# Writing the fourth chunk's result into the neighbouring image's slot, and storing five chunks with one DMA

## The chip, the cores and the metric

The kernel runs on one NeuronCore of a Trainium2 chip. The metric is the device time in microseconds (us) of one execution. Five engines work side by side, each through its own list of instructions in order: PE (matrix products), DVE (elementwise work), ACT (activation functions), POOL (elementwise work, and a queue of DMAs) and SP (a queue of DMAs). They meet through semaphores alone. A DMA is issued by an engine's queue (SP or POOL here) and carried out by 16 DMA engines that all queues share; its completion is counted on a semaphore, on which a later instruction can wait.

## The reference

Two layers are added to an image batch `x` of 16 images, 128 channels, 64 x 64 pixels, in float32. The first is a diagonal LSTM over the group-normalised input. The second, in which the change lies, is a 1 x 1 convolution through a simulated four-qubit circuit:

```python
x = x + _L0_conv_ref(_gn(x), ...)          # diagonal LSTM
x = x + _L1_conv_ref(_gn(x), ...)

def _L1_conv_ref(x, pre_w, pre_b, q_weights, post_w, post_b):
    xq = xf @ pre_w.T + pre_b              # 128 channels -> 4 angles per pixel
    z = _simulate(xq, q_weights)           # 4 qubits, 2 layers -> 4 expectations
    out = z @ post_w.T + post_b            # 4 -> 128 channels
    ...
```

The result has the shape of `x`: 16 images of 128 x 4096 float32, 2 MB each.

## The kernel before

**Where the data lies.** The 128 channels are the 128 partitions. An image's 4096 pixels are eight chunks of 512 (`CHUNK`), numbered k = 0 to 7 in the order of its rows. On the chip, `ring` (line 111) holds for each of the 16 images 40 of the 64 rows, that is five chunks of 2 KB a partition. Its rows are turned: `place` (line 140) puts k = 4, 5, 6, 7 into the first four chunks of an image's slot, and k = 3 into the fifth and last. So within one image's slot k = 3 lies behind k = 7. As the slots lie one behind the other, the last chunk of image b-1's slot lies directly in front of image b's k = 4. The three lower chunks (k = 0, 1, 2; `NT` is 3) do not fit and wait in a DRAM tensor `low` (line 114). They are brought back into buffers that come free: first into those of the first stage, then, as images are finished, into the places of their k = 4, 5, 6 in `ring` (`freed`, `load`, lines 1071 to 1088).

**The stages.** First the input is loaded and its statistics are taken. Then comes a scan of 160 steps (`NSTEP`), which takes most of the time. The last stage begins about 1277 us after the start of the span and handles the images one after another. It is written out by hand (`tc.manual_schedule()`, line 1233), so each engine works in the order in which the code emits instructions. The loop at line 1272 does this for image b:

- `outputs(b, 0)`: four matmuls on PE, each with 32 rows of the array, into four PSUM banks of a pool of five (`ps_o`, line 1060): results `po` for k = 0 to 3.
- `finish(b, 0)`: for each k one DVE instruction (line 1196) adds the bias and the old value and writes the sum back over that old value; then its store is issued, where one is due (line 1207, SP's queue).
- `load()`: loads of lower chunks for later images, on POOL's queue, for each buffer that came free.
- `sines(b + 2)` in two parts: ACT and one DVE instruction (line 1151); between the parts `squares(b + 1)`: two PE matmuls (line 1162) and two squares on ACT (line 1175).
- `outputs(b, 1)` and `finish(b, 1)`: the same for k = 4 to 7.
- `angles(b + 3)`: eight PE matmuls (line 1120) that read all eight chunks of image b + 3.
- In the last images, where no angles are left, `idle` puts two matmuls in their place whose results nobody reads.

**Which stores go together.** `together` (line 1216) says how many chunks one store carries. From image 5 to image 14 an image makes three stores: k = 0 to 2 in one (768 KB; two stores for image 5, whose three lie in two buffers), k = 3 alone (256 KB), and k = 4 to 7 in one (1024 KB). In the last image k = 4 to 7 go as two stores of 512 KB. A DMA on SP's queue uses one of eight completion semaphores in turn, and waits for the DMA eight before it.

Of the kernel before, what the change touches and what calls it, by code (L numbers as in the profile page):

```python
# [13 lines left out]
ALU = mybir.AluOpType  # L14
# [3 lines left out]
NB = 16  # L18
NH = 64
NW = 64  # L20
# [3 lines left out]
RING = 40  # L24
ROWS = 4
BLOCK = ROWS * NW
CHUNK = 2 * BLOCK
# [55 lines left out]
def kernel(  # L83
# [16 lines left out]
    nc = tc.nc  # L100
    xv = x.rearrange("b c h w -> b c (h w)")
    ov = out.rearrange("b c h w -> b c (h w)")
# [8 lines left out]
    ring = const.tile([P, NB, RING * NW], F32, name="ring")  # L111
    NLOW = NH - RING
    NT = NLOW * NW // CHUNK
# [24 lines left out]
    b_out = const.tile([P, 1], F32, name="b_out")  # L138

    def place(r):  # L140

        return (r + AHEAD if r < SLOTS else r - SLOTS) * NW

    def block(r):

        return ring[:, :, place(r) : place(r) + BLOCK]
# [18 lines left out]
    with ExitStack() as scan:  # L165
# [68 lines left out]
        with ExitStack() as prep:  # L234
# [37 lines left out]
            def behind(b):  # L272
# [10 lines left out]
                out=qw, in_=q_weights.rearrange("l w a -> (l w a)").partition_broadcast(P)  # L283
# [703 lines left out]
        with tc.manual_schedule():  # L987
# [26 lines left out]
            v = block(NH - ROWS).rearrange("p i (r w) -> p i r w", w=NW)[:, :, :, NW - STRIP :]  # L1014
# [55 lines left out]
    begun = {5: (last[:, 1:2], 1)}  # L1070
    freed, loaded = [], [len(groups)]

    def load():

        while freed and loaded[0] < NB:
            b = loaded[0]
            groups[b] = freed.pop(0)
            k = 0
            if b in begun:
                v, k = begun[b]  # L1080
                groups[b] = [(groups[b][0][0][:, k:], NT - k)]
            for v, n in groups[b]:
                of = low[b, :, k * CHUNK : (k + n) * CHUNK]
                nc.gpsimd.dma_start(out=v, in_=of.rearrange("p (k n) -> p k n", n=CHUNK))
                k += n
            if b in begun:
                groups[b].insert(0, begun[b])
            loaded[0] += 1

    def low_group(b, k):  # L1090

        for v, n in groups[b]:
            if k < n:
                return v, n, k
            k -= n

    def rows_of(b, k):
        if k < NT:
            v, _, i = low_group(b, k)
            return v[:, i]  # L1100
        at = place(2 * ROWS * k)
        return ring[:, b, at : at + CHUNK]

    def half(v, c):

        if c is None:
            return v
        return v[:, c * BLOCK : (c + 1) * BLOCK]
# [68 lines left out]
    def outputs(b, h, c=None, js=range(4)):  # L1177
        po = []
        for j in js:
            po.append(half(bank(ps_o, f"po{b}_{h}_{j}_{c}"), c))  # L1180
            k = 32 * j
            nc.tensor.matmul(  # L1182
                po[-1],
                lhsT=w_out[k : k + 32, :],
                rhs=half(sqs[b][h], c)[k : k + 32, :],
                start=True,
                stop=True,
                tile_position=(k, 0),
            )
        return po  # L1190

    def finish(b, h, po, c=None):
        for j in range(4):
            k = 4 * h + j
            v = rows_of(b, k)
            nc.vector.scalar_tensor_tensor(half(v, c), po[j], b_out, half(v, c), ALU.add, ALU.add)  # L1196
            n = together(b, k)
            if (k + 1) % n == 0 if k >= NT else n == 1 or n == low_group(b, k)[2] + 1:
                o = ov[b, :, (k + 1 - n) * CHUNK : (k + 1) * CHUNK].rearrange("p (k n) -> p k n", n=CHUNK)
                if k >= NT:  # L1200
                    at = place(2 * ROWS * (k + 1 - n))
                    to = ring[:, b, at : at + n * CHUNK].rearrange("p (k n) -> p k n", n=CHUNK)
                else:
                    to = v.unsqueeze(1) if n == 1 else low_group(b, k)[0]
                if c is not None:
                    o, to = (u[:, :, c * BLOCK : (c + 1) * BLOCK] for u in (o, to))
                nc.sync.dma_start(out=o, in_=to)
            if c != 0:
                if k == NT - 1 and len(groups[b]) == 1:
                    freed.append(groups[b])  # L1210
                if k == 7:
                    at = place(8 * ROWS)
                    v = ring[:, b, at : at + NT * CHUNK]
                    freed.append([(v.rearrange("p (k n) -> p k n", n=CHUNK), NT)])

    def together(b, k):

        if k < NT:
            return low_group(b, k)[1] if b > 1 else 1
        if k == NT:  # L1220
            return 1
        return 2 if b < 4 or b == NB - 1 else 4
# [10 lines left out]
    with tc.manual_schedule():  # L1233
# [15 lines left out]
        angles(1, 1, th, (0,))  # L1249
        po = outputs(0, 0, 0)  # L1250
        finish(0, 0, po, 0)
        squares(0, 1)
        angles(1, 1, th, (1,))
        ths[1, None] = th
        po = outputs(0, 0, 1)
        finish(0, 0, po, 1)
        load()
        later = sines(1)
        next(later)
        th = angles(2, parts=(0,))  # L1260
        po = outputs(0, 1, 0)
        finish(0, 1, po, 0)
        next(later, None)
        angles(2, None, th, (1,))
        po = outputs(0, 1, 1)
        finish(0, 1, po, 1)
        load()
        later = sines(2)
        next(later)
        squares(1)  # L1270
        next(later, None)
        for b in range(1, NB):
            po = outputs(b, 0)
            if b == 1:
                finish(b, 0, po)
                load()
                squares(2)
                th = angles(3, parts=(0,))
                po = outputs(b, 1)
                angles(3, None, th, (1,))  # L1280
                finish(b, 1, po)
                load()
                later = sines(3)
                next(later)
                next(later, None)
                continue
# [9 lines left out]
            po = outputs(b, 1)  # L1296
# [43 lines left out]
```

## Time and profile before

| what | value |
|---|---|
| three runs | 1395.71, 1396.30, 1396.86 us, median 1396.3 |
| profiled execution, its own time | 1396.12 us |
| its span, first to last instruction | 1394.3 us |
| mean granted TensorE clock | 0.994 |
| 1304 to 1390 us of the span: busy PE / DVE / ACT / POOL | 78.98 / 77.49 / 34.50 / 4.23 of 86.00 us |
| 1304 to 1390 us: what the DMA engines moved | 36.11 MB, 420 GB/s |
| stores of 1024 KB there, issue to landing (median) | 13.1 us |
| first stores of the stage (128 KB), issue to landing | 1.7 to 1.8 us |

The span is what the profiler saw between the first and the last instruction; the execution's own time has 1.8 us around it. Times inside the span are given from its start. A DMA's time to landing runs from its issue until the last of the 16 engines has counted its share; with a long queue most of it is waiting behind earlier DMAs. "Busy" for PE takes modelled ends of matmuls, so it says little about how full the array is. The clock is given as a share of full speed.

### The profile page before, as it was taken

To read this page: it belongs to the slowest core of one execution; us is meant where nothing else is said; L and a number is where in the kernel's file an instruction comes from. 1 tells how busy PE (TensorE), PEld (TensorE's weight loads), DVE (VectorE), ACT (ScalarE), POOL (GpSimd) and SP (SyncE) were. 2 spreads that over 40 slices of the span, in tenths; PEclk is the share of its full clock that TensorE was granted. 3 is DMA by queue.
4 is the path that set the end of the run, shared out by engine and by line. 5 is a ranking of instruction groups with operands and counts; after the bars stand their busy time and mean duration, and the time that the engine had idled before them with its cause. 6 is when DMAs were issued, how large, how long until landed. Compare 5 with 4: busy or idle time off the path is not lost. (4 is left out here: it accounts for less than half of the span.)

```text
span 1394.3 us, 19810 instructions
## 1 busy us (share of the span) xinstructions
PE 1348.3 (97%) x6058; PEld 966.7 (69%) x6058; DVE 970.3 (70%) x2509; ACT 796.1 (57%) x1896; POOL 876.3 (63%) x1560
## 2 busy tenths in 40 slices
PE   7888999999999999999999999999999999999996
PEld 6668878777777777767777777777777778886332
DVE  6973565577767776677777776666665566876996
ACT  6765666555555555555555555555555556655542
POOL 3236777776666677777777776777777667664000
PEclk9999999999999999999999999999999999999998
DMA  9950000000000000133333100000000000013999
GB/s 370 418 204 1 2 1 1 1 1 1 1 1 1 0 1 1 61 122 122 121 121 121 61 1 0 1 1 0 1 1 1 1 0 1 1 31 129 373 420 376
DMA packets 47674, 107.02 MB, mean 77 GB/s; under 512 B 2976, under 2 KB 30656, under 8 KB 44496
## 3 DMA queue, kind: packets, MB, share of 16 engines
q1 hardware_dynamic: 44928, 95.17, 18.1%
q0 software_dynamic: 2496, 10.58, 2.1%
q8 instruction: 48, 0.79, 0.2%
q14 instruction: 58, 0.48, 0.1%
q10 hardware_dynamic: 144, 0.01, 0.0%
HBM read 59.61 MB, written 46.14 MB: 76 GB/s over the span
## 5 line engine op out<-in xcount | busy, mean ns | idle before, releaser
L694 PE MATMUL ps<-trio,wxT 128*128 128x512 f32 (+18 forms) x1280 | 479.6, 518 | 0.6 <-POOL trio L685 0.6
L888 DVE TENSOR_TENSOR ps<-ps,both 128x256 f32<-128x256 f32 (+9 forms) x536 | 219.8, 410 | 295.4 <-PE ps L873 291.1
L892 ACT ACTIVATE ps<-ps,bias 128x512 f32<-128x512 f32 (+23 forms) x480 | 279.2, 583 | 219.4 <-DVE ps L888 183.1
L694 PEld LDWEIGHTS ps<-trio,wxT 128*128 128x128 f32 x1280 | 230.9, 190 | 173.2 <-issue 155.5
L873 PE MATMUL ps<-trio,w1T 128*128 128x256 f32 (+14 forms) x1088 | 306.3, 363 | 0.0
L873 PE MATMUL ps<-trio,w0T 128*128 128x256 f32 (+14 forms) x1088 | 305.5, 362 | 0.0
L923 ACT COPY both<-ps 128x256 f32<-128x256 f32 (+9 forms) x536 | 189.8, 356 | 180.9 <-PE ps L873 161.4
L873 PEld LDWEIGHTS ps<-pair,wsT 128*128 128x128 f32 x1088 | 196.0, 190 | 78.7 <-DVE pair L958 30.4
L873 PE MATMUL ps<-pair,wsT 128*128 128x256 f32 (+14 forms) x1088 | 243.5, 365 | 1.6 <-DVE pair L958 1.3
L731 POOL TENSOR_TENSOR ring<-ring,pair 128x256 f32<-128x256 f32 (+15 forms) x375 | 232.0, 646 | 18.2 <-DVE pair L958 17.9
L873 PEld LDWEIGHTS ps<-trio,w1T 128*128 128x128 f32 x1088 | 201.6, 190 | 22.3
L873 PEld LDWEIGHTS ps<-trio,w0T 128*128 128x128 f32 x1088 | 201.1, 190 | 21.2
L685 POOL TENSOR_TENSOR trio<-trio,rstd 128x512 f32<-128x512 f32 (+10 forms) x160 | 171.1, 1070 | 14.2 <-DVE rstd L529 1.7
L679 POOL TENSOR_TENSOR trio<-ring 128x256 f32<-128x256 f32 (+13 forms) x165 | 140.4, 851 | 0.0
L952 ACT ACTIVATE g<-cst 128x256 f32<-128x256 f32 (+20 forms) x320 | 103.0, 368 | 64.1 <-DVE cst L951 63.5
L958 DVE TENSOR_TENSOR pair<-g,ps 128x256 f32<-128x256 f32 (+17 forms) x319 | 105.4, 368 | 44.3 <-ACT g L952 39.4
L721 POOL TENSOR_TENSOR trio<-pair 128x240 f32<-128x240 f32 (+9 forms) x136 | 102.9, 757 | 36.6 <-DVE pair L958 33.0
L673 POOL TENSOR_TENSOR trio<-ring,mean 128x256 f32<-128x256 f32 (+15 forms) x191 | 123.3, 646 | 2.5 <-DVE mean L518 2.0
L978 POOL COPY trio<-pair 128x16 f32<-128x16 f32 x64 | 21.1, 330 | 148.7 <-DVE pair L958 148.7
L892 ACT ACTIVATE g<-ps,bias 128x512 f32<-128x512 f32 (+20 forms) x160 | 97.4, 609 | 27.6 <-DVE ps L888 21.4
L951 DVE TENSOR_TENSOR cst<-cst,ps 128x256 f32<-128x256 f32 (+20 forms) x320 | 104.4, 367 | 5.5
L948 DVE TENSOR_TENSOR ps<-ps,g 128x512 f32<-128x512 f32 (+20 forms) x160 | 95.0, 594 | 18.7 <-ACT g L892 18.5
(389 smaller groups left out, 1226.0 us busy)
## 6 DMA issues: line engine op xcount, KB each, us to landing
ring<-in_x_dram SPq DMA_DIRECT2D x13, 1024.0 KB, 9.8
low<-ring SPq DMA_DIRECT2D x6, 2048.0 KB, 7.6
ring<-in_x_dram SPq DMA_DIRECT2D x6, 2048.0 KB, 8.0
out_dram<-ring SPq DMA_DIRECT2D x11, 1024.0 KB, 13.1
trio<-in_x_dram SPq DMA_DIRECT2D x7, 768.0 KB, 7.6
rest<-in_x_dram SPq DMA_DIRECT2D x7, 768.0 KB, 7.7
ring<-low POOLq DMA_DIRECT2D x7, 768.0 KB, 8.9
out_dram<-ring SPq DMA_DIRECT2D x7, 768.0 KB, 12.7
```

What stands on the lines that cost most here:

```text
L673: op = nc.gpsimd.tensor_sub(by_pairs(xn, 0, j0, j1), x0, over(mean1, j1 - j0))
L679: op = nc.gpsimd.tensor_sub(by_pairs(xn, 1, j0, j1), lower, of)
L685: nc.gpsimd.tensor_mul(v, v, r)
L694: nc.tensor.matmul(ps[g][:, :, a:b], lhsT=wxT[:, g * 128 : (g + 1) * 128], rhs=xns[t % 2][:, :, a:b], start=t > 0, stop=True, skip_group_c ...
L731: op = engine.tensor_add(x1, x1, by_pairs(new, q, j0, j1))
L873: nc.tensor.matmul(out, lhsT=w[:, g * 128 : (g + 1) * 128], rhs=rhs, start=False, stop=True, skip_group_check=True,)
L888: nc.vector.tensor_add(v, v, both[g][:, a:b])
L892: nc.scalar.activation(to[:, :, a:w], ps[g][:, :, a:w], FUNC[g], bias=bias[:, g : g + 1])
L923: nc.scalar.copy(both[g][:, a:b], ps[g][:, 0, a:b])
L951: nc.vector.tensor_add(c[:, q], c[:, q], ig[:, q])
L952: nc.scalar.activation(th[:, q, a:w], c[:, q], AF.Tanh)
L958: nc.vector.tensor_mul(new[:, q, a:v], th[:, q, a:v], act[GO][:, q, a:v])
```

## The change

For the images 5 to 14 (`joined`), DVE's result for k = 3 no longer goes back over its own old value in the fifth chunk of image b's slot, but into the fifth chunk of image b-1's slot. There it stands directly in front of k = 4 to 7 of image b. k = 3 has no store of its own any more; when k = 7 is done, one DMA of 1280 KB stores k = 3 to 7, 10240 contiguous bytes a partition on both sides. Images 0 to 4 and 15 are as before.

```diff
     begun = {5: (last[:, 1:2], 1)}
     freed, loaded = [], [len(groups)]
 
+    flat = ring.rearrange("p b n -> p (b n)")
+    size = RING * NW
+    joined = {b: flat[:, b * size - CHUNK : b * size + (7 - NT) * CHUNK] for b in range(5, NB - 1)}
+
     def load():
...
         for j in range(4):
             k = 4 * h + j
             v = rows_of(b, k)
+            if b in joined and k == NT:
+                to = joined[b][:, 0:CHUNK]
+                nc.vector.scalar_tensor_tensor(to, po[j], b_out, v, ALU.add, ALU.add)
+                continue
             nc.vector.scalar_tensor_tensor(half(v, c), po[j], b_out, half(v, c), ALU.add, ALU.add)
             n = together(b, k)
-            if (k + 1) % n == 0 if k >= NT else n == 1 or n == low_group(b, k)[2] + 1:
+            if b in joined and k == 7:
+                nc.sync.dma_start(out=ov[b, :, NT * CHUNK : 8 * CHUNK], in_=joined[b])
+            elif (k + 1) % n == 0 if k >= NT else n == 1 or n == low_group(b, k)[2] + 1:
                 o = ov[b, :, (k + 1 - n) * CHUNK : (k + 1) * CHUNK].rearrange("p (k n) -> p k n", n=CHUNK)
```

The numbers and kinds of instructions on PE, DVE, ACT and POOL are the same in both programs; SP issues ten DMAs less. Semaphore waits are put in by the framework, from which instruction touches which bytes.

## The prediction

> **What bounds the kernel now.** The change touches the last stage alone, so I first read the table of stretches there, with the DMA columns; one row is a stretch of the span, its length, busy time of each engine, the granted clock, the DMA engines' share and GB/s.
>
> ```profile
> 1304.00:1390.00 86.00, 78.98 (x428) 27.07 (x424) 77.49 (x117) 34.50 (x58) 4.23 (x8) 0.96 1.02 420
> 1389.00:1390.70 1.70, 0.00 (x0) 0.00 (x0) 0.00 (x0) 0.00 (x0) 0.00 (x0) 0.50 0.85 346
> ```
>
> From 1304 to 1390 us the DMA engines are never idle. PE stops at 1383 and DVE at 1385.1 (its last eight operations start at 1379.74 and take 5.36 together), yet DMA goes on. SP's waits say how long:
>
> ```profile
> SPq L1336 <- DMA out_dram<-ring: 6.9, 1, 6.9
> ```
>
> So the span ends with the landing of the last store. It is issued at 1385.12 and lands 7.86 us later, at 1392.98; 1.3 us behind it the span ends. The first stores of the stage, of 128 KB, land in 1.7 us. What would the last one take without a queue before it? The trace's DMA packets give the service: a row of 2048 bytes holds its engine for 84 ns, 4096 for 159, 6144 for 234, 8192 for 309, that is 9 ns and 75 ns per 2 KB, and each DMA has 8 rows per engine and a 4-byte packet of 9 ns. Image 15's stores (768, 256, 512 and 512 KB, the first issued at 1381.83) therefore take 1.88 + 0.68 + 1.28 + 1.28 = 5.1 us; with a fixed 1.4 us (1.7 less 8 rows of half a 2 KB row, about 0.37 us) they would land at 1381.83 + 5.1 + 1.4 = 1388.4. **The store queue is thus 4.6 us behind the engines at the end** (1392.98 - 1388.4). This is the number to beat: engines that run up to 4.6 us later cost nothing, as long as the queue stays fed.
>
> What paces the engines is the next question. The timeline of DVE around image 5 (start, duration, operation; in brackets the idle time before it and who ended it):
>
> ```profile
> 1317.76 0.75 DVE L1196 SCALAR_TENSOR_TENSOR last<-po_None,b_out,last 128x512 f32<-128x512 f32 x1 [0.23 <-PE po_None L1182]
> 1318.42 1.40 DVE L1196 SCALAR_TENSOR_TENSOR trio<-po_None,b_out,trio 128x512 f32<-128x512 f32 x2
> 1319.74 0.74 DVE L1196 SCALAR_TENSOR_TENSOR ring<-po_None,b_out,ring 128x512 f32<-128x512 f32 x1
> 1320.40 0.68 DVE L1151 SCALAR_TENSOR_TENSOR y<-near_None,y 128x512 f32<-128x512 f32 x1
> 1321.00 2.72 DVE L1196 SCALAR_TENSOR_TENSOR ring<-po_None,b_out,ring 128x512 f32<-128x512 f32 x4
> 1323.94 2.73 DVE L1196 SCALAR_TENSOR_TENSOR ring<-po_None,b_out,ring 128x512 f32<-128x512 f32 x4 [0.23 <-PE po_None L1182]
> ```
>
> An image takes 6.18 us (1317.76 to 1323.94), with 0.23 us of idle DVE. PE is in the same loop: `po` of k = 0 to 3 is ready 1.16 us after its start, three DVE operations (2.07) free the bank for the eighth `po`, that takes 1.1, and the angles 1.85; the sum is 6.18. So neither engine can catch up by more than a fraction of 0.23 us an image.
>
> **What the change does, part by part.** *Ten stores less on SP.* A row of 10240 bytes costs 9 + 5 x 75 = 384 ns by the line above, against 84 + 309 = 393 for the two rows, so per engine and image 8 x 9 ns, and 9 for the packet that counts the completion: 81 ns, 0.8 us over ten images. No row that long is in the trace. If it is cut into 8192 and 2048, 0.1 us is left; if into five of 2048, it costs 420 ns and DMA loses 10 x (8 x 27 - 9) ns = 2.1 us. I take -0.8, as four lengths lie on the line. SP's own time, 0.33 us an issue, is hidden: it spends 38.1 us waiting for DVE here.
>
> *k = 3 is stored 4.1 us later* (1324 instead of 1320): behind stores that take 13 us to land this starves nobody. The buffers that come free for loads (k = 4 to 6) hung on the 1024 KB store and hang on the 1280 KB one, which is at the same place of the queue. The loads of images 14 and 15, issued at 1338.6 and 1340.8, land by 1352.1; the angles of 14 read them at about 1358, so they have 6 us of cover, and the delay below moves both.
>
> *A DVE operation writes elsewhere.* It keeps its 0.74 us: `last`, `trio` and `ring` targets all have it. For images 6 to 14 the chunk written over is the old k = 3 of the image before, whose readers are PE's angles and DVE's own earlier operation; it no longer has a store of its own. **For image 5 it is the place from which image 4's k = 3 is stored**, and this is new: the program of the changed kernel shows a wait for that store's semaphore on this operation, and on no other k = 3. The listing of this one store:
>
> ```profile
> L1207 SPq DMA_DIRECT2D out_dram<-ring x1: 951/951/951, 1314.3 to 1314.3; - x1
> ...
> DMA to landing us min/median/max: 10.7/10.7/10.7
> ```
>
> Issued at 1314.32, it lands at 1325.06. DVE wants to write at 1319.74: **5.3 us of standstill**. Nothing ahead of that store changes, so its landing is as certain as the queue's state. Behind the waiting instruction on DVE stand line 1151 of image 7, for which ACT waits with image 6's squares, and the four operations of k = 4 to 7. PE has banks for image 5's upper four and finishes image 8's angles at 1322.8; then it waits: the banks come free only from 1325.8 on, and the squares of image 6 need line 1151 (done 1326.5) and 0.6 us of ACT. So PE stands from 1322.8 to 1327.1. Walking on with the durations above, DVE begins image 6 at 1329.2 (before: 1323.94), image 7 at 1335.3 (1330.13) and then stays 5.2 us late. DMA has work meanwhile: at 1325 image 4's 1024 KB, image 5's 768 KB and loads 10 to 12 are still in the queue, and stores issued at 1319.85 land at 1333; it falls idle only in the images after, 1 us at a time, as it runs out of backlog.
>
> Against the 4.6 us of cover this alone is 1388.4 + 5.2 = 1393.6, or +0.6 us.
>
> *The clock of PE.* What does PE do after 4.3 us of standstill? The same table, in stretches of 6.83 us, the step on which all the clock's changes in this trace lie:
>
> ```profile
> 4.67:11.49 6.82, 4.28 (x30) 3.66 (x29) 3.65 (x7) 3.81 (x12) 5.79 (x18) 1.00 1.01 369
> 11.49:18.32 6.83, 4.53 (x20) 4.15 (x21) 5.71 (x10) 2.82 (x10) 0.38 (x3) 0.50 1.06 402
> 18.32:25.15 6.83, 5.59 (x40) 4.69 (x40) 5.62 (x10) 5.89 (x24) 1.49 (x5) 1.00 1.03 422
> 1288.08:1294.90 6.82, 6.14 (x40) 2.12 (x40) 5.64 (x11) 4.07 (x7) 0.53 (x1) 1.00 0.86 259
> 1322.21:1329.04 6.83, 6.83 (x47) 2.16 (x39) 6.60 (x11) 3.58 (x7) 0.53 (x1) 1.00 1.01 418
> 1376.82:1383.65 6.83, 6.16 (x20) 2.08 (x20) 5.94 (x10) 0.00 (x0) 0.00 (x0) 1.00 1.02 422
> 1383.65:1390.48 6.83, 0.00 (x0) 0.00 (x0) 1.45 (x3) 0.00 (x0) 0.00 (x0) 0.50 0.99 408
> ```
>
> A stretch with 4.28 us of busy PE is followed by one at half clock; so is one with 6.16 us, in which the last `po` came one by one, while 6.14 us of denser work kept the clock. With the wait, the stretch from 1322.21 has 0.6 us of angles and 1.9 us of `po`, again one by one: 2.5 of 6.83, far under both that lost it. I take one stretch at half clock. PE loses at most half of it, 3.4 us; while DVE is still catching up, about 0.6 of that lies beside DVE's work, as PE then only waits for banks. That leaves 2.8 us. The bounds: nothing, if no stretch loses its clock; 0.6 if the half clock begins at 1324 and mostly covers the standstill itself; 4.8 if it lasts two stretches.
>
> The Trainium skill, "TensorE: Matmul & The Clock Gate", part 1, gives a free-running window of about 3.4 us: after an idle one the array goes to half rate, and after a busy one it comes back. The rows agree that the clock is either 1.0 or 0.5, but change only on a step of 6.83. By the page a drop at 1325.6, cleared after two of its windows, would leave 1.4 us in place of 2.8 and the sum would be +2.0. "DMA: Bandwidth & Descriptors", Rules for kernel authors, advises coalescing and at least 1 MiB a DMA; here it speaks for the change, worth the 0.8 us above, which the wait takes away.
>
> *The sum.* 1388.4 + 5.2 + 2.8 = 1396.4 for the last landing, against 1392.98: +3.4. The queue's own end, 1392.98 - 0.8 = 1392.2, no longer decides. On the profiled execution's 1396.12 this makes **1399.5 us**. The median before is 0.2 above that execution, which I leave out.
>
> **Rivals.**
> *The clock holds.* +0.6, so 1396.7. For it: no stretch in this stage has lost its clock before PE ran out of work at 1383. Against it: none had a hole of over 1 us.
> *The wait is short and the store queue sets the end: faster.* If image 4's store lands by 1323.5, the delay is under 3.8 us (1392.2 - 1388.4) and the end is the queue's: -0.8, 1395.3. For it: the last engine counts that store 2.4 us behind the first (1322.68), so another execution may be earlier. Against it: all stores from 1313 on take over 10 us. More than 4.6 us (1392.98 - 1388.4) can't be gained.
> *Worse than one stretch.* A second stretch at half clock, 4.8 in place of 2.8, or a store landing at 1327: +5.4, 1401.5 and over.
>
> **How the numbers follow.** One stretch at half clock 0.67 (alone 1397.6 to 1400.6), clock holds 0.17, queue sets the end 0.09, worse 0.07. A measurement of this kernel can tell about 0.2%, 2.8 us, from no change: the border is 1399.1. A stretch that begins where this trace's steps lie is over it, an earlier one under it; I put 0.50 of the 0.67 over. Slower: 0.50 + 0.07 = 0.57. Faster: 0.05 of the 0.09, for a longer row cheaper than the line together with a short wait. The rest, 0.38, is within. The range goes from 1396.2, half a us under the case of the held clock, to 1401.8, a little over two stretches.
>
> **What would show it.** In the profile after: the image-5 operation waits 5 us for a DMA of `ring`, the only such wait; the next images are 5 to 8 us later; the granted clock shows a stretch at 0.5 near 1325 to 1336; stores near the end land in 3 to 5 us rather than 8 to 13; DMA shows holes from 1342 on; rows of 10240 bytes take 384 ns. It is wrong if that wait is under 4 us, if the last stores still take 8 us (then the queue still decides), or if the clock stays at 1.0.

## The result and the profile after

The changed kernel takes 1399.64 us (median of 11 runs, 1399.12 to 1400.73), the one before 1396.45 (11 runs, 1395.71 to 1396.96): ratio 1.0024, 95% interval 1.0016 to 1.0032. It is 3.2 us slower, a little over the 2.8 us that the prediction took as the least that can be told from no change. The profiled execution took 1399.12 us, with a span of 1397.4.

First the timeline of DVE at image 5 in the changed kernel (start, duration, operation, idle time before it and who ended it), the answer to the same lines of before:

```profile
1317.49 0.75 DVE L1204 SCALAR_TENSOR_TENSOR last<-po_None,b_out,last 128x512 f32<-128x512 f32 x1 [0.23 <-PE po_None L1186]
1318.15 1.40 DVE L1204 SCALAR_TENSOR_TENSOR trio<-po_None,b_out,trio 128x512 f32<-128x512 f32 x2
1325.87 0.75 DVE L1202 SCALAR_TENSOR_TENSOR ring<-po_None,b_out,ring 128x512 f32<-128x512 f32 x1 [6.32 <-DMA out_dram<-ring]
1326.54 0.68 DVE L1155 SCALAR_TENSOR_TENSOR y<-near_None,y 128x512 f32<-128x512 f32 x1
```

Line 1202 is the new write of k = 3. It stands 6.32 us for the DMA that stores image 4's k = 3 from that place; before, the same operation began 1.98 us after image 5's first, now 8.38 us after it. In all of the last stage it is DVE's only long wait for a DMA. What that does to PE stands in PE's timeline (its listing counts each of these matmuls twice: x8 are the four of `outputs`):

```profile
1320.66 1.92 PE L1124 MATMUL theta_None<-ring,w_image 128*32 128x512 f32 x16
1327.96 3.36 PE L1186 MATMUL po_None<-sq,w_out 32*128 32x512 f32 x8 [5.38 <-ACT sq L1179]
1331.25 2.08 PE L1166 MATMUL am_None<-y,w_amp 64*128 64x512 f32 x4
```

PE has nothing to do for 5.38 us. What follows is slow: line 1166 takes 2.08 us. In the kernel before, where it is line 1162, it took 1.13:

```profile
1324.16 1.13 PE L1162 MATMUL am_None<-y,w_amp 64*128 64x512 f32 x4
```

The reason is in the table of stretches (length, busy time of PE, weight loads, DVE, ACT, POOL, granted clock, DMA share, GB/s):

```profile
1304.00:1386.00 82.00, 76.62 (x412) 26.27 (x408) 71.35 (x109) 34.10 (x57) 4.22 (x8) 0.96 0.98 396
1320.95:1327.77 6.82, 1.63 (x16) 0.26 (x8) 1.90 (x3) 0.46 (x1) 0.53 (x1) 1.00 1.02 423
1327.77:1334.60 6.83, 6.64 (x20) 2.51 (x20) 5.41 (x9) 3.56 (x8) 0.53 (x1) 0.50 1.04 417
1334.60:1341.43 6.83, 6.83 (x44) 2.21 (x44) 6.18 (x10) 1.93 (x4) 1.05 (x2) 1.00 1.01 378
```

In the stretch before 1327.77 PE is busy for 1.63 of 6.82 us; the next stretch has half the clock. At its end it comes back and stays until PE's work is done. And the store queue? SP's wait at the end was 6.9 us; now its line (us in total, times, longest) and the landing of the last four stores (their listing's last line) read:

```profile
SPq L1346 <- DMA out_dram<-ring: 2.7, 3, 1.2
```

```profile
DMA to landing us min/median/max: 3.4/3.5/3.6
```

Before, these four stores took 7.9 to 8.1 us. So the queue has no backlog left. The first row of the table has 396 GB/s instead of 420, and the busy share of the DMA engines in 40 slices from 1304 to 1386 us, in tenths, shows them falling idle now and then; before, every slice to 1390 us was a 9:

```profile
DMA  9999999999999999999999999999999699599499
```

The engines set the end in place of the queue. The last landing is at 1396.38 (before: 1392.98).

### The profile page after: what moved, and what is told of

The parts are those of the page before. It is cut to its first block, busy times and chain, and to the rows that moved or that the text cites. A ratio compares the mean times of both kernels' runs of the same rounds, so it can differ in the third digit from the quotient of the medians.

```text
span 1397.4 us, 19791 instructions
## 1 busy us (share of the span) xinstructions
PE 1352.6 (97%) x6058; PEld 968.9 (69%) x6058; DVE 971.2 (70%) x2509; ACT 795.8 (57%) x1896; POOL 874.7 (63%) x1560
## 5 line engine op out<-in xcount | busy, mean ns | idle before, releaser
L685 POOL TENSOR_TENSOR trio<-trio,rstd 128x512 f32<-128x512 f32 (+10 forms) x160 | 170.9, 1068 | 14.2 <-DVE rstd L529 1.7
```

What stands on the lines that cost most here:

```text
L685: nc.gpsimd.tensor_mul(v, v, r)
```

## Experiments

Executions differ by up to 1.2 us in where the stage begins, so I compare delays from image 5's first DVE operation on. "DVE late" is how much later than before DVE's last operation of the kernel starts, "landing late" the same for the last store's landing, from the traces' starts and landings. In the profile before these two lie 66.60 and 75.23 us behind image 5's first operation.

| kernel | median, us | that operation's wait, us | half clock | DVE late | landing late |
|---|---|---|---|---|---|
| changed | 1399.64 | 6.3 | 6.83 us | 8.1 | 3.7 |
| wait alone | 1399.49 | 5.4 | 6.83 us | 7.5 | 2.8 |
| PE filled | 1397.21 | 6.3 | none | 6.1 | 1.7 |
| from image 8 on | 1406.26 | 12.0 | 13.65 us | 14.2 | 9.8 |
| 3 operations more | 1396.51 | none | none | 2.0 | -0.1 |
| 8 operations more | 1399.63 | none | 10.24 us | 8.4 | 3.8 |
| shift from image 1 on | 1395.18, again 1395.17 | none | none | 0.0 | -0.5, again -0.5 |
| that without merging | 1396.41 | none | none | 0.0 | 0.3 |

The half clock is the one between 1320 and 1365 us. The kernel before ran beside them with medians of 1396.46 (the four kernels of the first batch: shift from image 1, wait alone, PE filled, from image 8) and 1396.23 (the others). All ratios below are to it. "From image 8 on" has 4 runs, the others 10 or 11. The diffs are against the changed kernel where nothing else is said.

**The wait alone.** Nothing is merged; image 5 alone writes one chunk to the left and stores it from there.

```diff
-    joined = {b: ... for b in range(5, NB - 1)}
+    joined = {b: ... for b in (5,)}
...
                 nc.vector.scalar_tensor_tensor(to, po[j], b_out, v, ALU.add, ALU.add)
+                nc.sync.dma_start(out=ov[b, :, NT * CHUNK : (NT + 1) * CHUNK], in_=to)
                 continue
...
-            if b in joined and k == 7:
-                nc.sync.dma_start(out=ov[b, :, NT * CHUNK : 8 * CHUNK], in_=joined[b])
-            elif (k + 1) % n == 0 ...
+            if (k + 1) % n == 0 ...
```

> The wait alone: the kernel before, but image 5's k = 3 is written into image 4's slot and stored alone from there; no store is merged. Theory A: the same stand of 5 to 6.5 us at image 5, a stretch at half clock behind it, and the full loss: 1399 to 1400.5 us (+2.5 to +4). Theory B (the loss is in the merged stores): 1396.0 to 1396.8, no change.

Measured: 1399.49 us, ratio 1.0022 (1.0012 to 1.0031). One place that one operation writes to makes the whole loss. Its DVE timeline and the stretch at half clock:

```profile
1325.14 0.75 DVE L1202 SCALAR_TENSOR_TENSOR ring<-po_None,b_out,ring 128x512 f32<-128x512 f32 x1 [5.39 <-DMA out_dram<-ring]
```

```profile
1320.71:1327.53 6.82, 2.37 (x19) 0.71 (x20) 2.39 (x4) 0.95 (x2) 1.06 (x2) 1.00 1.01 415
1327.53:1334.36 6.83, 6.83 (x20) 2.01 (x17) 4.88 (x8) 3.56 (x7) 0.53 (x1) 0.50 1.03 425
```

**Shift from image 1 on.** The chain of shifts begins where the neighbour's store has long landed; the ten wide stores stay. From image 2 on, each writes over a chunk that has no store of its own.

```diff
-    joined = {b: ... for b in range(5, NB - 1)}
+    joined = {b: ... for b in range(1, NB - 1)}
...
                 nc.vector.scalar_tensor_tensor(to, po[j], b_out, v, ALU.add, ALU.add)
+                if b < 5:
+                    nc.sync.dma_start(out=ov[b, :, NT * CHUNK : (NT + 1) * CHUNK], in_=to)
                 continue
...
-            if b in joined and k == 7:
+            if b in joined and b >= 5 and k == 7:
```

> Shift from image 1 on: each image from 1 to 14 writes its k = 3 into the slot before it, images 1 to 4 store it alone from there, images 5 to 14 store five chunks in one as in the changed kernel. Only image 1 then waits for a store (image 0's, which landed 5 us earlier). Theory A (the cost is the one wait and the clock it takes away): no DVE operation waits over 0.5 us for a DMA after 1300 us, no stretch at half clock near 1330, and the store queue sets the end again, 0.8 us earlier than before: about 1395.6 us, 1395.0 to 1396.4. Theory B (the wide store itself costs, through later stores or long rows): still 1399 to 1400.

Measured: 1395.18 us, ratio 0.9991 (0.9982 to 1.0000). No DVE operation waits for a DMA after 1300 us. The table's row for the stage and SP's wait at the end:

```profile
1304.00:1389.00 85.00, 78.94 (x428) 27.06 (x424) 77.46 (x117) 34.42 (x58) 4.22 (x8) 0.98 1.02 422
```

```profile
SPq L1348 <- DMA out_dram<-ring: 6.1, 5, 1.8
```

DMA never idles, SP waits 6.1 us at the end: the queue sets the end again, and the wide stores themselves cost nothing. I ran it again beside the same kernel without the merging, whose diff against the shift from image 1 on is:

```diff
-                if b < 5:
+                if b:
                     nc.sync.dma_start(out=ov[b, :, NT * CHUNK : (NT + 1) * CHUNK], in_=to)
...
-            if b in joined and b >= 5 and k == 7:
-                nc.sync.dma_start(out=ov[b, :, NT * CHUNK : 8 * CHUNK], in_=joined[b])
-            elif (k + 1) % n == 0 ...
+            if (k + 1) % n == 0 ...
```

> The shift of k = 3 from image 1 on without any merged store: each image from 1 to 14 stores its k = 3 alone, from the slot before its own. If the gain of the shift from image 1 on comes from the merged stores (0.8 us by the packets, 1.3 measured), this one is as the kernel before: 1396.45 within 0.4 us. If it comes from the place that is written: 1395.2.

> The shift from image 1 on with merged stores, once more beside the kernel without them: 1395.2 within 0.5 us, 0.8 to 1.4 us under the kernel before and under the shift alone.

Measured: 1396.41 without merging, ratio 1.0001 (0.9992 to 1.0009); 1395.17 with it, 0.9994 (0.9985 to 1.0002). The two merged runs agree, and lie 1.2 us under the unmerged one, 1.1 to 1.3 under the kernel before. That is less than a measurement of this kernel tells with certainty: one interval ends at 1 and the other goes past it. Against the changed kernel, at 1399.64, the gain of 4.5 us is plain. It is the fastest version here, though its lead over the kernel before is not proved.

**PE filled.** The changed kernel with four matmuls ahead of image 8's angles, whose results nobody reads.

```diff
+            if b == 5:
+                idle()
+                idle()
             if b + 3 < NB:
                 angles(b + 3)
```

> The changed kernel with four matmuls more on PE ahead of image 8's angles (two calls of idle(), 3.8 us), so that PE has work while DVE waits. Theory A with the clock as a part of the cost: the wait on DVE stays at 5 to 6.5 us, the clock stays at 1.0, and the end comes 1.8 to 2.8 us earlier than the changed kernel's: 1396.8 to 1398.0 us. Rival (the half clock is hidden beside DVE's catching up, the wait alone makes the loss): 1399.3 to 1400, as the changed kernel.

Measured: 1397.21 us, ratio 1.0004 (0.9995 to 1.0013), 2.4 us under the changed kernel. (Its runs go from 1395.38 to 1398.30. The profiled one is the slowest; its stage began 1.2 us later than that of the changed kernel's profile.) PE's timeline, and the table's stretches of the same length as the clock's:

```profile
1321.82 1.98 PE L1239 MATMUL I-10836_10837<-w_image,w_out 128*128 128x512 f32 x4
1323.87 1.98 PE L1239 MATMUL I-10840_10841<-w_image,w_out 128*128 128x512 f32 x4
1325.91 1.92 PE L1124 MATMUL theta_None<-ring,w_image 128*32 128x512 f32 x16
1329.16 2.41 PE L1186 MATMUL po_None<-sq,w_out 32*128 32x512 f32 x8 [1.33 <-ACT sq L1179]
1331.50 1.13 PE L1166 MATMUL am_None<-y,w_amp 64*128 64x512 f32 x4
```

```profile
1321.90:1328.73 6.83, 5.81 (x24) 1.69 (x24) 1.66 (x3) 0.22 (x1) 0.74 (x2) 1.00 1.02 423
1328.73:1335.56 6.83, 6.40 (x36) 2.20 (x36) 6.83 (x12) 3.86 (x8) 0.53 (x1) 1.00 1.04 422
```

PE's hole is 1.33 us instead of 5.38, the clock stays at 1.00, line 1166 takes 1.13 again, and DVE still waits its 6.3 us. So the half clock is a cost of its own: 2.0 us of DVE's delay (8.1 against 6.1). Most of it shows in one place. In the changed kernel DVE stands once more, for PE, before image 6's upper four; with PE filled it stands nowhere in that image:

```profile
1335.07 2.73 DVE L1204 SCALAR_TENSOR_TENSOR ring<-po_None,b_out,ring 128x512 f32<-128x512 f32 x4 [1.67 <-PE po_None L1186]
```

**From image 8 on.** The same change, begun three images later, where the queue is longer.

```diff
-    joined = {b: ... for b in range(5, NB - 1)}
+    joined = {b: ... for b in range(8, NB - 1)}
```

> The same change from image 8 on in place of 5. Theory A: the wait is the landing time of image 7's k = 3 store less 6.2 us of one image. Before, that store is issued at 1332.9 and lands at 1349.6, image 8's k = 3 is due at 1338.3: 11.2 us of standstill, then a stretch at half clock worth about 2 us: last landing near 1388.4 + 11 + 2 = 1401.5, time about 1404.5 us, 1402.5 to 1407. Theory B (cost per merged store or row): seven merged images in place of ten, so 0.7 of the loss: about 1398.7 us.

Measured: 1406.26 us, ratio 1.0069 (1.0055 to 1.0082). Three merged images less, three times the loss. Timeline of DVE and table:

```profile
1351.05 0.75 DVE L1202 SCALAR_TENSOR_TENSOR ring<-po_None,b_out,ring 128x512 f32<-128x512 f32 x1 [12.04 <-DMA out_dram<-ring]
```

```profile
1346.99:1360.65 13.66, 7.51 (x24) 2.70 (x28) 7.41 (x12) 4.51 (x8) 0.00 (x0) 0.50 0.80 332
```

The wait is 12.0 us, near the 11.2 that the landing time of that store gave. The time is 1.8 us over the expected value, within its bounds; 1.2 us of that are DVE's delay, 14.2 us where the expectation added up 11 and 2, most of it the longer wait. The half clock lasts twice as long as in the changed kernel, but 4.1 of its 13.65 us lie in the wait itself, and what DVE is late beyond the wait is 2.2 us.

**DVE delayed without any DMA.** The kernel before, with three or eight operations more just ahead of image 5's k = 3. They write into the last chunk of image 1's slot, which nobody reads any more.

```diff
+            if b == 5 and k == NT:
+                over = ring[:, 1, 4 * CHUNK : 5 * CHUNK]
+                for _ in range(3):
+                    nc.vector.scalar_tensor_tensor(over, po[j], b_out, v, ALU.add, ALU.add)
             nc.vector.scalar_tensor_tensor(half(v, c), po[j], b_out, half(v, c), ALU.add, ALU.add)
```

> The kernel before, with three DVE operations more just ahead of image 5's k = 3 (the same operation, written into a place whose store is long done; nobody reads it): DVE stands back by 3 times 0.75 to 0.85, 2.2 to 2.6 us, with no DMA changed and no wait added. If the 4.6 us by which the store queue trails the engines are cover, as the prediction has it, the time stays: 1396.45 within 0.5 us. If every us of DVE's delay comes out at the end: 1398.7 to 1399.0.

> As the kernel with three operations more, but eight: 6.0 to 6.8 us, about the standstill of the changed kernel, again without any DMA changed. Theory A: it costs what the wait costs. The delay passes the 4.6 us of cover, and if PE loses its clock for a stretch, the end is 1388.4 + 6.2 + 1.8 = 1396.4 for the last landing, 1399.5 us, 1398.0 to 1400.5. If the loss needs the stores to be held back or merged: 1396.5.

Measured: 1396.51 us with three, ratio 0.9998 (0.9989 to 1.0006); 1399.63 with eight, 1.0025 (1.0015 to 1.0034). The inserted operations in the two timelines, three first:

```profile
1319.91 2.32 DVE L1199 SCALAR_TENSOR_TENSOR ring<-po_None,b_out,ring 128x512 f32<-128x512 f32 x3
```

```profile
1319.48 6.25 DVE L1199 SCALAR_TENSOR_TENSOR ring<-po_None,b_out,ring 128x512 f32<-128x512 f32 x8
```

2.3 us of DVE vanish without a trace; 6.3 us cost what the wait costs, clock included. With three, PE's hole was 1.33 us and its clock held, at 1.00 until the end of PE's work:

```profile
1324.36 2.41 PE L1182 MATMUL po_None<-sq,w_out 32*128 32x512 f32 x8 [1.33 <-ACT sq L1175]
```

The table above then gives the cover directly. DVE late less landing late, before rounding, is 4.45 (changed), 4.63 (wait alone), 4.48 (PE filled), 4.47 (from image 8) and 4.63 us (eight operations). Whatever made DVE late, the first 4.4 to 4.6 us of it were free.

## Why the prediction was right

1399.5 us was forecast, 1399.64 measured, and the steps were those forecast; two sizes in the sum were off and cancelled. That the number came out within 0.2 us is luck.

- **The cover**, 4.6 us between queue and engines: 4.4 to 4.6 us in five kernels, and a delay of 2.0 us under it cost nothing. Right. (Its fixed 1.4 us is 1.7 less 0.37, which is 1.33; with that the cover would have been put at 4.7.)
- **The one wait**, on image 4's store and at image 5 only: right, shown by the wait alone making the loss and by its absence from the shift from image 1 on. Its size, 5.3 us, was too small in the changed kernel: 6.3. The store landed at 1325.78 instead of 1325.06 and the stage began 0.27 us earlier; the kernel with the wait alone had 5.4. The step treated one execution's landing as fixed. In the traces of the ten kernels this store takes 10.7 to 11.8 us from issue to landing, and the 10.7 of the kernel before is the shortest.
- **What is behind it**: PE's standstill was put at 1322.8 to 1327.1 and came as 1322.6 to 1328.0. The loop does not catch up: forecast 0.1 us of 5.3 regained, measured 6.1 us left of 6.3 (PE filled).
- **The clock**: one stretch at half clock, as forecast, and the rival in which the clock holds fell with the PE-filled kernel. Its price was put at 2.8 us and is 2.0. PE was busy for 6.64 us at half clock and so lost 3.3; 1.3 of that, not 0.6, lay beside DVE's own work. Why it was more is not shown; the stretch did begin 1.3 us sooner than the step of the trace before would have it. That the price goes by the length of the stretch, as the bound of 4.8 us for two stretches has it, is not borne out. DVE late less its own delay is 1.8, 2.1, 2.1 and 2.2 us for stretches of 6.83, 6.83, 10.24 and 13.65 us; the rows show PE busy for 6.6 to 7.6 us in all four.
- So the sum 5.2 + 2.8 = 8.0 us for DVE was 6.1 + 2.0 = 8.1.
- **The stores**: a row of 10240 bytes takes 385 ns in the trace of the changed kernel, 384 by the line. The 0.8 us forecast for the queue's end is measured, where the wait is gone, as 1.1 to 1.3 us in time and 0.5 us in the profiled landing; that spread is larger than the term.
- **The rival on the other side**, in which the queue sets the end: its price, 1395.3, is what the shift from image 1 on has (1395.2). It needed the delay under 3.8 us, and the wait was 6.3.
- One of the signs was wrong: DMA was said to show holes from 1342 on; they begin near 1368, so the backlog lasted longer than the prediction had it.
- Two readings were off without weight in the sum: k = 3 is stored 3.1 us later, not 4.1 (the stores are issued at 1320.63 and 1323.74), and of the stores from 1313 on the last eight take 7.9 to 9.8 us, not over 10.

The Trainium skill, "TensorE: Matmul & The Clock Gate", part 1, with its window of about 3.4 us, was set against a step of 6.83 us that the trace before showed. The runs since speak for the page's window: half-clock stretches of 10.24 and 13.65 us, three and four times 3.41, and one of 3.42 early in the changed kernel's span.

## What to carry to other kernels

A buffer that is written to save a DMA may still be the source of an earlier one: look up when that one lands, not when it was issued; in a full queue the wait is the store's time to landing, less the time until the next write is due (6.3 and 12.0 us here, for stores that took 11.7 and 17.4 us to land and a write that was due 5.4 us after their issue), and a chain of such shifts pays it once, at its first link, so begin the chain where the queue is short. Where a queue of stores sets the end, work out how far it trails the engines: that many us of engine delay are free (about 4.5 here), and only what goes past them costs. A PE that stands still may cost again afterwards by its clock, 2.0 us here; four matmuls without a reader were cheaper.

## What was not expected of the hardware

The step on which the clock changes is not fixed to the start of the span, and is finer than the trace before showed. Early in the changed kernel's span, and then in the kernel with eight operations more, the table of stretches reads:

```profile
13.64:17.06 3.42, 3.26 (x16) 2.86 (x14) 2.74 (x5) 2.18 (x8) 0.37 (x3) 0.50 1.04 405
```

```profile
1318.36:1325.19 6.83, 4.23 (x28) 1.19 (x24) 6.58 (x10) 0.24 (x1) 1.06 (x2) 1.00 1.02 425
1325.19:1335.43 10.24, 7.58 (x24) 2.72 (x28) 8.02 (x13) 4.50 (x8) 0.53 (x1) 0.50 1.02 418
```

The second pair shows the clock lost at 1325.19 after 2.6 us of idle PE (its angles end at 1322.6), while the kernel with three operations more kept it over a hole of 1.33 us. Taken in steps of 3.41 us, the last step before the loss holds 0.81 us of busy PE with eight operations more and none in the changed kernel, while the step with most of the hole holds 2.09 us with three operations more, and the clock stays. Busy time alone does not decide it: in the kernel before, 2.74 us with 7 matmul entries (1380.24 to 1383.65) were followed by half clock, and 2.73 us with 20 (1288.08 to 1291.49) were not. How long a hole has to be, and how a sparsely filled array counts, was not tried.
